# A gated mLSTM and mixture-of-experts layer on one core: row normalization on ScalarE, a shorter logarithm for the gates, other queues for the first loads, a third buffer for context rows

## The chip, the core and the metric

The kernel runs on one core of a Trainium2 chip. The core has five engines with a queue of instructions each: TensorE (PE in the profile; its weight loads are PEld), VectorE (DVE), ScalarE (ACT), GpSimd (POOL) and SyncE (SP). An engine takes its instructions in order and waits at each one until the semaphores that it needs have been raised. SP issues most transfers between the chip's memory (HBM) and the on-chip memory (SBUF); ACT and POOL can issue transfers as well. TensorE writes its products into PSUM, in tiles of which there are few.

The metric is the time of one execution on the device in microseconds (us), lower is better. The kernel before takes 3212.82 us, the median of 3 runs (3210.32 to 3215.99).

## What is computed

The input x has 8 sequences of 512 tokens of width 1024, and a context of the same shape. All is float32. With tokens in rows, for each sequence:

```
xn    = layernorm(x)                                   # over the 1024 columns
gates = [xn, ctx, ctx] @ [Wi | Wf] + [bi | bf]         # 16 input and 16 forget gates a token
logf  = log_sigmoid(forget gate); cum = cumsum(logf)   # along the sequence
D     = exp(cum_s - cum_t + i_t - max over t)          # t <= s, for each of 16 heads
C     = (xn_h @ ctx_h^T) / 8 * D                       # heads of width 64
h     = C / max(|sum C|, exp(-max)) @ ctx_h            # then normalized per head, scaled
x1    = x + tanh(g_xattn) * h
y     = layernorm(x1)
out   = x1 + tanh(g_ffn) * (shared(y) + routed(y))     # SwiGLU networks
```

`shared` is a SwiGLU network of width 1024 for all tokens; `routed` sends each token to the best 2 of 16 experts of width 512 by a router's softmax and sums their outputs with the two weights.

## The kernel before

The 4096 tokens are 32 tiles of 128 rows. The work has two parts, and the first is the one that the change touches.

**Attention part (lines 306 to 926, up to about 1450 us).** The loop at line 856 goes over the tiles i. One iteration holds pieces of three tiles: the last steps of tile i-1 (`head_norm`, `finish_rows`, `turn_rows`, routing), the scores and values of tile i, and the first steps of tile i+1 (`prep_queries`, `prep_keys`, `gate_products`, `prep_gates`, `prep_columns`), with the loads and the normalization of tile i+2. So that TensorE does not wait, units of the shared network for tiles already finished are laid between these pieces: `fill(share)` takes units from a queue, each 16 matmuls of 128x256 (lines 248) or half the down projection (line 265), about 7 us of TensorE for two of them.

The chain of a tile through the engines is this:

- The x row arrives by SP (line 321), the context row kv as well (line 326, two buffers).
- `row_stats` (lines 120 to 127): two `bn_stats` and one `bn_aggr` on DVE give mean and variance. `inverse_deviation` (lines 111 to 118): two operations on POOL give 1/sqrt(variance + eps). `normed` (line 426): one DVE operation subtracts the mean and multiplies. This is done for x (`prep_norm`) and again for x1 (`finish_rows`), 64 times in all.
- The normalized row is transposed on TensorE, eight 128x128 blocks in two PSUM tiles of tag "tr" (line 408), and copied out by ACT (qT, line 409). The same is done with kv, copied out by DVE (kT), and later with y (yT). Tag "tr" has two buffers, which these transposes share with the gates' products and `prep_columns`.
- `gate_products` and `prep_gates` (lines 455 to 525): the products `pp` are copied by ACT (`parts`, line 421), summed by one more matmul (`pg`, line 464), and worked on in 16x128 rows by DVE and ACT: the forget gate f (line 471), its bias (473), z = min(-f, f), exp(z) on ACT (478), u = 1 + exp(z), its logarithm on ACT (480), and then nine DVE operations (481 to 489). They correct the logarithm by z/(u - 1), which takes a reciprocal, and by a comparison for u = 1. Two scans give cum and the running maximum m, and nm = -m (line 501).
- nm goes to HBM and comes back broadcast to all partitions as the tile `d` (lines 505 and 506); exp of m goes the same way as `eb` (lines 513 to 520). POOL cuts the upper triangle of d (line 535).
- `prep_columns` transposes the gates' rows (`pc`, line 530); DVE copies them to `cols` (line 532), takes the decay out of eb (541) and multiplies eb by the queries (542). POOL forms wv (line 550).
- 16 exponentials on ACT (line 577), with cols as bias, turn d into D; DVE multiplies it with the scores (line 593); the values follow on TensorE (lines 608 and 614).

The order of the instructions on each engine is set by a scheduler when the program is built, from the order in the source and the tiles' dependences. `tc.issue_after(ins)` keeps what is written under it behind `ins`. `pinned(order, after)` does the same for an instruction handed on; `behind` holds the last matmul of the last unit of `fill`.

**Start (lines 86 to 424 and 810 to 851).** Constants are set on POOL; SP loads x and kv of tiles 0 and 1 and the input gates' weights `wi`; ACT's queue issues the loads of the two gates, `wf`, the two biases, `lnsc`, the router's weights and the zeros into the last rows of `acc_d`. Then the first tile goes through the chain alone.

**Expert part (lines 994 to 1446, from about 1450 us).** The experts' products, at line 1281, with the same instructions before and after.

Of the kernel before, what the change touches and what calls it, by code (L numbers as in the profile page):

```python
# [9 lines left out]
F32 = mybir.dt.float32  # L10
# [8 lines left out]
P = 128  # L19
S = 512  # L20
D = 1024
# [21 lines left out]
def flamingo_layer(  # L43
# [47 lines left out]
    mhalf = const.tile([P, NH], F32, name="mhalf")  # L91
    nc.gpsimd.memset(mhalf, -0.5)
    gates_t = const.tile([P, 2], F32, name="gates_t")
    nc.scalar.dma_start(gates_t[:, 0:1], g_xattn.unsqueeze(0).to_broadcast([P, 1]))
    nc.scalar.dma_start(gates_t[:, 1:2], g_ffn.unsqueeze(0).to_broadcast([P, 1]))
    tg = const.tile([P, 2], F32, name="tg")
    nc.scalar.activation(tg, gates_t, AF.Tanh)
    tgx, tgf = tg[:, 0:1], tg[:, 1:2]
# [21 lines left out]
    def row_stats(pool, row):  # L120

        st = pool.tile([P, 2, 6], F32, tag="bst", name="bst")
        for k in range(2):
            nc.vector.bn_stats(st[:, k, :], row[:, k * 512 : (k + 1) * 512])
        mv = pool.tile([P, 2], F32, tag="bmv", name="bmv")
        nc.vector.bn_aggr(mv, st.rearrange("p a b -> p (a b)"))  # L126
        return mv
# [178 lines left out]
    with ExitStack() as actx:  # L306
# [15 lines left out]

        def load_kv(i: int):
            q, b, c = toks[i], i // NS, i % NS
            q.kv = wk.tile([P, D], F32, tag="kv", name="kv")
            nc.sync.dma_start(q.kv, ctx_in[b, c * P : (c + 1) * P, :])

        load_x(0)
# [3 lines left out]

        w3 = wk.tile([P, 3 * NC, 32], F32, tag="sq", name="w3", bufs=1)
        nc.sync.dma_start(w3[:, :, 0:NH], wi.rearrange("(c p) h -> p c h", p=P))
        nc.scalar.dma_start(w3[:, :, NH:], wf.rearrange("(c p) h -> p c h", p=P))
        bias_i = ac.tile([NH, 1], F32, name="bias_i")
        bias_f = ac.tile([NH, 1], F32, name="bias_f")
        nc.scalar.dma_start(bias_i, bi.unsqueeze(1))
        nc.scalar.dma_start(bias_f, bf.unsqueeze(1))
        ones_p = ac.tile([P, P], F32, name="ones_p")  # L340
        nc.gpsimd.memset(ones_p, 1.0)
        ones = ones_p[:NH, :]
# [11 lines left out]
        ltop = ac.tile([P, 2, NT], F32, name="ltop")  # L354

        lnsc = ac.tile([P, D], F32, name="lnsc")
        nc.scalar.dma_start(lnsc, ln_scale.unsqueeze(0).to_broadcast([P, D]))


        sums = ac.tile([P, 48], F32, name="sums")  # L360
# [15 lines left out]
        state = ac.tile([P, NH // 2, 2 * (DH + 1)], F32, name="state")  # L376
        nc.gpsimd.memset(state, 0.0)
        zeros = state.rearrange("p c e -> p (c e)")
        nc.scalar.dma_start(acc_d[T : T + P, :], zeros[:, :D])
        zero80 = ac.tile([P, NT_], F32, name="zero80")  # L380
        nc.gpsimd.memset(zero80, 0.0)
        uptos = [ac.tile([P, 5, NE], F32, name=f"upto{k}") for k in range(2)]
# [10 lines left out]
        def prep_router():  # L393
            nc.vector.tensor_scalar(lnsc, lnsc, tgx, None, ALU.mult)
            rw = wk.tile([NE, D], F32, tag="u", name="rw", bufs=1)
            nc.scalar.dma_start(rw, router_w)
            nc.vector.memset(rwT, 0.0)
            prw = ps.tile([P, NC, NE], F32, tag="tr", name="prw")
            for c in range(NC):
                nc.tensor.transpose(prw[:, c, :], rw[:, c * P : (c + 1) * P], ident[:NE, :NE])  # L400
            nc.scalar.copy(rwT[:, :, 0:NE], prw)
# [19 lines left out]
            nc.scalar.copy(parts, pp)  # L421
            return parts

        def normed(row, mean, rstd):
            o = wk.tile([P, D], F32, tag="row", name="row", bufs=2)
            normed.last = nc.vector.tensor_scalar(o, row, mean, rstd, ALU.subtract, ALU.mult).ins
            return o

        def prep_norm(i: int):
            q = toks[i]  # L430
            mv = row_stats(sm, q.x)
            rstd = inverse_deviation(sm, mv[:, 1:2], LN_EPS, [P, 1])
            q.xn = normed(q.x, mv[:, 0:1], rstd)

        def prep_values(i: int):
            q = toks[i]
# [22 lines left out]
        def prep_gates(i: int, after=()):  # L459
            q, last, first = toks[i], i % NS == NS - 1, i % NS == 0  # L460
            pg = ps.tile([48, P], F32, tag="tr", name="pg")
            with ExitStack() as order:
                pinned(order, after)
                nc.tensor.matmul(pg, lhsT=sums, rhs=q.parts, start=True, stop=True)

            def row(name, bufs=2):
                return gt.tile([NH, P], F32, tag=name, name=name, bufs=bufs)

            f = row("f", 1)
            a, en, w = (rows3[i % 2][32 * k : 32 * k + NH, :] for k in range(3))  # L470
            nc.scalar.copy(f, pg[32:48, :])
            nc.vector.tensor_scalar(a, pg[0:NH, :], bias_i, None, ALU.add)
            nc.vector.tensor_scalar(f, f, bias_f, None, ALU.add)


            z, u, lnu, eq = (row(n, 1) for n in ("z", "u", "lnu", "eq"))
            nc.vector.scalar_tensor_tensor(z, f, -1.0, f, ALU.mult, ALU.min)
            nc.scalar.activation(z, z, AF.Exp)
            nc.vector.tensor_scalar(u, z, 1.0, None, ALU.add)
            nc.scalar.activation(lnu, u, AF.Ln)  # L480
            nc.vector.tensor_scalar(u, u, -1.0, None, ALU.add)
            nc.vector.tensor_scalar(eq, u, 0.0, None, ALU.is_equal)
            nc.vector.tensor_add(u, u, eq)
            nc.vector.reciprocal(u, u)
            nc.vector.tensor_mul(u, u, z)
            nc.vector.tensor_mul(lnu, lnu, u)
            nc.vector.tensor_mul(eq, eq, z)
            nc.vector.tensor_add(lnu, lnu, eq)
            nc.vector.scalar_tensor_tensor(f, f, 0.0, lnu, ALU.min, ALU.subtract)

            q.cum, q.m = row("cum"), row("m")
            before = None if first else toks[i - 1]
            nc.vector.tensor_tensor_scan(
                q.cum, ones, f, 0.0 if first else before.cum[:, P - 1 : P], ALU.mult, ALU.add
            )
            nc.vector.tensor_sub(a, a, q.cum)
            nc.vector.tensor_tensor_scan(
                q.m, a, a, LOWEST if first else before.m[:, P - 1 : P], ALU.max, ALU.max
            )
            nm = row("nm", 1)  # L500
            nc.vector.tensor_scalar(nm, q.m, -1.0, None, ALU.mult)
# [21 lines left out]
            nc.scalar.activation(en, en, AF.Exp, scale=-1.0)  # L523
            if not last:
                nc.scalar.activation(w, a, AF.Exp, bias=nm[:, P - 1 : P])

        def prep_columns(i: int):
            q, last, first = toks[i], i % NS == NS - 1, i % NS == 0
            pc = ps.tile([P, 5, NH], F32, tag="tr", name="pc")
            nc.tensor.transpose(pc.rearrange("p k h -> p (k h)"), rows3[i % 2], ident[:80, :80])  # L530
# [146 lines left out]
        def finish_rows(i: int):  # L677
            q = toks[i]
            nc.sync.dma_start(x1_d[i] if i < NT - 4 * HELD else acc_d[i * P : (i + 1) * P, :], q.x)
            mv = row_stats(sm, q.x)  # L680
            rstd = inverse_deviation(sm, mv[:, 1:2], LN_EPS, [P, 1])
            q.y = normed(q.x, mv[:, 0:1], rstd)
            nc.sync.dma_start(y_d[i * P : (i + 1) * P, :], q.y)

        def turn_rows(i: int):
# [126 lines left out]
        prep_norm(0)  # L812
        prep_queries(0)
        prep_keys(0)
        with tc.issue_after(normed.last):
            prep_gate_weights()
            prep_values(0)
        gate_products(0)
        prep_gates(0)
        prep_columns(0)  # L820
        with tc.issue_after(normed.last):
            prep_norm(1)
        with tc.issue_after(normed.last):
            prep_router()
        prep_weights(0, 0)
        prep_weights(0, 1)
# [16 lines left out]
        nc.sync.dma_start(sh_down, sh_down_w.rearrange("(c p) d -> p c d", p=P))  # L843
        prep_values(1)
        load_x(2)
        prep_columns(1)
        load_kv(2)
        route_products(0)
        finish_route(0)
        fill()  # L850
# [5 lines left out]
        for i in range(1, NT):  # L856
# [622 lines left out]
```

## Time and profile before

| What | Value |
|---|---|
| time, median of 3 runs | 3212.82 us |
| the profiled execution: time | 3221.06 us |
| its span, first to last instruction | 3219.3 us |
| granted TensorE clock, mean over the span | 0.975 |
| TensorE busy | 3107.8 us, 97% |
| VectorE busy | 1798.4 us, 56% |
| ScalarE busy | 863.7 us, 27% |
| GpSimd busy | 1295.2 us, 40% |

The profile is of one execution. Its page has, for each engine, the busy time and the number of instructions, the busy share in 40 equal slices, and the costliest groups of instructions by line of the code with their tiles as "out<-in". The trace behind it answers more: the busy time by stretch, the waits ("engine, line <- what it waited for: total us, times, longest us"), and the instructions in order of time. A wait for several semaphores is put down to the one that came last. Matmuls are pipelined and their ends are modelled, so short gaps of TensorE are not exact.

### The profile page before, as it was taken

What the parts mean: (1) busy time and instruction counts of PE and PEld (TensorE: products, weight loads), DVE (VectorE), ACT (ScalarE), POOL (GpSimd) and SP (SyncE); (2) the same over time, 40 slices, a digit from 0 to 9 for tenths busy, and PEclk for the clock granted to TensorE, in tenths of its full rate; (3) what the DMA queues carried; (4) which work ended last, traced back from release to release, by engine and by line L of the source; (5) the groups of instructions that cost most, each with busy time, mean ns of one, the idle gap of its engine ahead of it and who ended that gap; (6) DMA issues with size and microseconds to landing.
All of it is one profiled execution on the core that took longest, in us unless ns stands there. A gap on an engine that the chain in (4) does not pass through costs nothing.

```text
span 3219.3 us, 42324 instructions
## 1 busy us (share of the span) xinstructions
PE 3107.8 (97%) x16127; PEld 2294.8 (71%) x16127; DVE 1798.4 (56%) x3573; ACT 863.7 (27%) x1825; POOL 1295.2 (40%) x993
## 2 busy tenths in 40 slices
PE   6999989999999999999999999999999999999999
PEld 5778777786877867666666666666677777776666
DVE  5655666767667675644444444444454445455554
ACT  3444444443544544311111111111111111100000
POOL 2213232323231323235555555555565544444342
PEclk7889999999999999999999999999999999999999
DMA  6766565666656666553544545444454544645330
GB/s 191 206 210 190 174 181 171 191 187 187 197 170 191 184 188 174 161 198 130 141 121 115 141 134 136 122 119 128 129 142 135 141 129 131 187 163 173 106 130 27
DMA packets 371280, 501.52 MB, mean 156 GB/s; under 512 B 24352, under 2 KB 262480, under 8 KB 366944
## 3 DMA queue, kind: packets, MB, share of 16 engines
q1 hardware_dynamic: 342560, 425.00, 42.1%
q0 software_dynamic: 24752, 72.44, 10.8%
q8 instruction: 130, 2.13, 0.3%
q10 hardware_dynamic: 3760, 1.31, 0.2%
q14 instruction: 78, 0.64, 0.1%
HBM read 394.57 MB, written 114.61 MB: 158 GB/s over the span
## 4 chain that ended last, share of the span: by engine, by line
PE 51%; DVE 3%; issue 0%; DVEq 0%
PE pq L1281 48%; PE ptx L1199 2%; PE pq L1382 1%; DVE hsum L1345 1%; DVE hsum L1346 1%; DVE hT L1303 1%; DVE up L1302 0%; DVE tsum L1230 0%; DVE tsum L1228 0%; DVE tsum L1227 0%; DVE yo L1356 0%; DVE hT L1347 0%; DVE u L1363 0%; DVE u L1362 0%; DVE xT L1202 0%
## 5 line engine op out<-in xcount | busy, mean ns | idle before, releaser
L1281 PE MATMUL pq<-xT,w 128*128 128x256 f32 (+1 forms) x2112 | 513.4, 393 | 8.5 <-DVEq L1262 8.5
L1281 PEld LDWEIGHTS pq<-xT,w 128*128 128x128 f32 x2112 | 401.7, 191 | 101.3 <-issue 13.4
L1281 PE MATMUL pq<-tsum,wsum 128*128 128x256 f32 (+1 forms) x1408 | 349.8, 391 | 0.0
L248 PE MATMUL pgu<-sh_yT,swg 128*128 128x256 f32 (+1 forms) x1280 | 299.2, 384 | 1.3 <-DMA swg<-L_ffn_shared_gate_w_dram 1.3
L1281 PEld LDWEIGHTS pq<-tsum,wsum 128*128 128x128 f32 x1408 | 264.0, 190 | 49.5
L265 PE MATMUL pso<-sh_down,sh_hT 128*128 128x512 f32 x640 | 286.8, 599 | 2.3 <-DVE sh_hT L254 2.3
L248 PE MATMUL pgu<-sh_yT,swu 128*128 128x256 f32 (+1 forms) x1280 | 278.1, 371 | 0.9 <-DMA swu<-n_L_ffn_shared_up_w_dram 0.9
L248 PEld LDWEIGHTS pgu<-sh_yT,swu 128*128 128x128 f32 x1280 | 235.3, 191 | 31.5 <-DMA swu<-n_L_ffn_shared_up_w_dram 1.1
L1305 DVE TENSOR_TENSOR hT<-pq,u 128x256 f32<-128x256 f32 (+1 forms) x176 | 77.2, 439 | 322.4 <-PE pq L1281 318.8
L248 PEld LDWEIGHTS pgu<-sh_yT,swg 128*128 128x128 f32 x1280 | 233.1, 197 | 33.5 <-issue 3.2
L114 POOL TENSOR_SCALAR ve<-bmv 128x1 f32<-128x1 f32 x64 | 15.6, 243 | 580.7 <-DVE bmv L126 578.5
L1246 POOL TENSOR_TENSOR wsum<-w 128x512 f32<-128x512 f32 x88 | 113.6, 1290 | 295.1 <-PE pq L1281 290.8
L265 PEld LDWEIGHTS pso<-sh_down,sh_hT 128*128 128x128 f32 x640 | 119.0, 192 | 136.8 <-issue 132.1
L1302 DVE TENSOR_TENSOR up<-pq,u 128x256 f32<-128x256 f32 (+1 forms) x176 | 77.1, 438 | 223.7 <-PE pq L1281 222.3
L1012 POOL DMA_INDIRECT acc_d<-yo,row_i x64 | 102.1, 1595 | 184.4 <-ACT yo L1374 70.4
L1281 PE MATMUL pq<-wd,hT 128*128 128x512 f32 x352 | 169.6, 597 | 6.9 <-DVE hT L1303 5.4
L1281 PE MATMUL pq<-xT,wsum 128*128 128x256 f32 (+1 forms) x704 | 174.9, 391 | 0.0
L1281 PE MATMUL pq<-tsum,w 128*128 128x256 f32 (+1 forms) x704 | 174.9, 391 | 0.0
L1306 ACT ACTIVATE hT<-hT 128x256 f32<-128x256 f32 (+1 forms) x176 | 75.4, 429 | 339.2 <-DVE hT L1305 339.2
L1281 PE MATMUL pq<-dsum,hT 128*128 128x512 f32 x352 | 165.4, 592 | 0.0
L1281 PE MATMUL pq<-dsum,hsum 128*128 128x512 f32 x352 | 165.4, 592 | 0.0
L1356 DVE TENSOR_TENSOR yo<-pq,u 128x512 f32<-128x512 f32 x176 | 118.9, 686 | 76.9 <-PE pq L1281 56.5
(265 smaller groups left out, 5478.4 us busy)
## 6 DMA issues: line engine op xcount, KB each, us to landing
swg<-L_ffn_shared_gate_w_dram SPq DMA_DIRECT2D x88, 512.0 KB, 5.0
swu<-n_L_ffn_shared_up_w_dram SPq DMA_DIRECT2D x88, 512.0 KB, 5.8
w<-in_L_ffn_gate_w_dram SPq DMA_DIRECT2D x16, 2048.0 KB, 9.8
w<-in_L_ffn_up_w_dram SPq DMA_DIRECT2D x16, 2048.0 KB, 9.9
wd<-in_L_ffn_down_w_dram SPq DMA_DIRECT2D x16, 2048.0 KB, 8.0
d<-nm_d SPq DMA_DIRECT2D x31, 1024.0 KB, 6.2
x_sb<-in_x_dram SPq DMA_DIRECT2D x32, 512.0 KB, 4.9
kv<-in_ctx_dram SPq DMA_DIRECT2D x32, 512.0 KB, 6.0
```

The source lines that it names most:

```text
L248: last = nc.tensor.matmul(pg[:, half, :n], lhsT=w[:, c, :], rhs=st["yT"][:, c, :n], start=(c == 0), stop=(c == NC - 1),)
L265: last = nc.tensor.matmul(po, lhsT=st["hT"][:, k, t * P : (t + 1) * P], rhs=sh_down[:, k, cols], start=(k == 0), stop=(k == 2 * NFC - 1),)
L1012: nc.gpsimd.indirect_dma_start(out=rows, out_offset=bass.IndirectOffsetOnAxis(ap=index, axis=0), in_=row, in_offset=None, compute_op=ALU.add,)
L1199: nc.tensor.transpose(pt[:, c, :], row[:, (half * 4 + c) * P : (half * 4 + c + 1) * P], ident)
L1246: nc.gpsimd.tensor_tensor(s1, a21, a22, ALU.add)
L1281: nc.tensor.matmul(out, lhsT=left[:, c, :], rhs=right[:, c, :], start=(c == 0), stop=(c == chunks - 1))
L1302: nc.vector.tensor_tensor(up, part, other, ALU.add)
L1303: nc.vector.tensor_tensor(out, out, up, ALU.mult)
L1305: nc.vector.tensor_tensor(out, part, other, ALU.add)
L1306: nc.scalar.activation(out, out, AF.Silu)
L1345: nc.vector.tensor_tensor(s1, a21, a22, ALU.add)
L1356: nc.vector.tensor_tensor(rows[t][:, halves[half]], part, other, ALU.add)
```

## The change

- `normed` becomes one ACT activation, out = row * rstd + shift, with a new POOL operation for shift = -mean * rstd.
- The copy of f on ACT adds the bias. The correction of the logarithm becomes (u - 1 - z), subtracted from it: no division and no comparison. Ten DVE operations become three.
- The loads of the gates, biases, `lnsc`, the router's weights and the store of zeros are issued by POOL; `wf` by SP.
- kv has three buffers, and `load_kv(i + 2)` stands beside `load_x(i + 2)` in the middle of the iteration.
- At the end of the iteration `fill(share)` comes ahead of `prep_columns(i + 1)`, whose transpose is pinned behind the last unit.
- At the start, what was kept behind the first normalized row is kept behind its statistics, or behind nm of the first tile.

```diff
     def row_stats(pool, row):
         for k in range(2):
-            nc.vector.bn_stats(st[:, k, :], row[:, k * 512 : (k + 1) * 512])
+            row_stats.last = nc.vector.bn_stats(st[:, k, :], row[:, k * 512 : (k + 1) * 512]).ins
...
-    nc.scalar.dma_start(gates_t[:, 0:1], g_xattn.unsqueeze(0).to_broadcast([P, 1]))
-    nc.scalar.dma_start(gates_t[:, 1:2], g_ffn.unsqueeze(0).to_broadcast([P, 1]))
+    nc.gpsimd.dma_start(gates_t[:, 0:1], g_xattn.unsqueeze(0).to_broadcast([P, 1]))
+    nc.gpsimd.dma_start(gates_t[:, 1:2], g_ffn.unsqueeze(0).to_broadcast([P, 1]))
...
-            q.kv = wk.tile([P, D], F32, tag="kv", name="kv")
+            q.kv = wk.tile([P, D], F32, tag="kv", name="kv", bufs=3)
...
-        nc.scalar.dma_start(w3[:, :, NH:], wf.rearrange("(c p) h -> p c h", p=P))
+        nc.sync.dma_start(w3[:, :, NH:], wf.rearrange("(c p) h -> p c h", p=P))
-        nc.scalar.dma_start(bias_i, bi.unsqueeze(1))
-        nc.scalar.dma_start(bias_f, bf.unsqueeze(1))
+        nc.gpsimd.dma_start(bias_i, bi.unsqueeze(1))
+        nc.gpsimd.dma_start(bias_f, bf.unsqueeze(1))
-        nc.scalar.dma_start(lnsc, ln_scale.unsqueeze(0).to_broadcast([P, D]))
+        nc.gpsimd.dma_start(lnsc, ln_scale.unsqueeze(0).to_broadcast([P, D]))
-        nc.scalar.dma_start(acc_d[T : T + P, :], zeros[:, :D])
+        nc.gpsimd.dma_start(acc_d[T : T + P, :], zeros[:, :D])
-            nc.scalar.dma_start(rw, router_w)
+            nc.gpsimd.dma_start(rw, router_w)
...
-        def normed(row, mean, rstd):
+        def normed(row, mv):
+            rstd = inverse_deviation(sm, mv[:, 1:2], LN_EPS, [P, 1])
+            shift = sm.tile([P, 1], F32, tag="shift", name="shift")
+            nc.gpsimd.tensor_scalar(shift, mv[:, 0:1], rstd, -1.0, ALU.mult, ALU.mult)
             o = wk.tile([P, D], F32, tag="row", name="row", bufs=2)
-            normed.last = nc.vector.tensor_scalar(o, row, mean, rstd, ALU.subtract, ALU.mult).ins
+            nc.scalar.activation(o, row, AF.Identity, scale=rstd, bias=shift)
             return o
...
-            nc.scalar.copy(f, pg[32:48, :])
+            nc.scalar.activation(f, pg[32:48, :], AF.Identity, bias=bias_f)
             nc.vector.tensor_scalar(a, pg[0:NH, :], bias_i, None, ALU.add)
-            nc.vector.tensor_scalar(f, f, bias_f, None, ALU.add)
...
             nc.scalar.activation(lnu, u, AF.Ln)
-            nc.vector.tensor_scalar(u, u, -1.0, None, ALU.add)
-            nc.vector.tensor_scalar(eq, u, 0.0, None, ALU.is_equal)
-            nc.vector.tensor_add(u, u, eq)
-            nc.vector.reciprocal(u, u)
-            nc.vector.tensor_mul(u, u, z)
-            nc.vector.tensor_mul(lnu, lnu, u)
-            nc.vector.tensor_mul(eq, eq, z)
-            nc.vector.tensor_add(lnu, lnu, eq)
-            nc.vector.scalar_tensor_tensor(f, f, 0.0, lnu, ALU.min, ALU.subtract)
+            nc.vector.scalar_tensor_tensor(u, u, -1.0, z, ALU.add, ALU.subtract)
+            nc.vector.scalar_tensor_tensor(f, f, 0.0, u, ALU.min, ALU.add)
+            nc.vector.tensor_sub(f, f, lnu)
...
-        def prep_columns(i: int):
+        def prep_columns(i: int, after=()):
...
-            nc.tensor.transpose(pc.rearrange("p k h -> p (k h)"), rows3[i % 2], ident[:80, :80])
+            with ExitStack() as order:
+                pinned(order, after)
+                nc.tensor.transpose(pc.rearrange("p k h -> p (k h)"), rows3[i % 2], ident[:80, :80])
...
-        with tc.issue_after(normed.last):
+        with tc.issue_after(row_stats.last):
             prep_gate_weights()
             prep_values(0)
...
-        with tc.issue_after(normed.last):
+        with tc.issue_after(toks[0].gated):
             prep_norm(1)
-        with tc.issue_after(normed.last):
             prep_router()
...
             if i + 2 < NT:
                 load_x(i + 2)
+                load_kv(i + 2)
             fill(share)
...
-            if i + 2 < NT:
-                load_kv(i + 2)
+            fill(share)
             if nxt:
-                prep_columns(i + 1)
-            fill(share)
+                prep_columns(i + 1, behind)
```

(`toks[i].gated` is the instruction at line 501 that writes nm.)

More of the change, by code (lines that the diff above doesn't have):

```diff
@@ L430, in prep_norm @@
             q = toks[i]
-            mv = row_stats(sm, q.x)
-            rstd = inverse_deviation(sm, mv[:, 1:2], LN_EPS, [P, 1])
-            q.xn = normed(q.x, mv[:, 0:1], rstd)
+            q.xn = normed(q.x, row_stats(sm, q.x))
         def prep_values(i: int):
@@ L470, in prep_gates @@
             a, en, w = (rows3[i % 2][32 * k : 32 * k + NH, :] for k in range(3))
-            nc.scalar.copy(f, pg[32:48, :])
+            nc.scalar.activation(f, pg[32:48, :], AF.Identity, bias=bias_f)
             nc.vector.tensor_scalar(a, pg[0:NH, :], bias_i, None, ALU.add)
-            nc.vector.tensor_scalar(f, f, bias_f, None, ALU.add)
-            z, u, lnu, eq = (row(n, 1) for n in ("z", "u", "lnu", "eq"))
+            z, u, lnu = (row(n, 1) for n in ("z", "u", "lnu"))
             nc.vector.scalar_tensor_tensor(z, f, -1.0, f, ALU.mult, ALU.min)
@@ L500, in prep_gates @@
             nm = row("nm", 1)
-            nc.vector.tensor_scalar(nm, q.m, -1.0, None, ALU.mult)
+            q.gated = nc.vector.tensor_scalar(nm, q.m, -1.0, None, ALU.mult).ins
             q.d = wk.tile([P, NH, P], F32, tag="d", name="d")
@@ L679, in finish_rows @@
             nc.sync.dma_start(x1_d[i] if i < NT - 4 * HELD else acc_d[i * P : (i + 1) * P, :], q.x)
-            mv = row_stats(sm, q.x)
-            rstd = inverse_deviation(sm, mv[:, 1:2], LN_EPS, [P, 1])
-            q.y = normed(q.x, mv[:, 0:1], rstd)
+            q.y = normed(q.x, row_stats(sm, q.x))
             nc.sync.dma_start(y_d[i * P : (i + 1) * P, :], q.y)
@@ L845, in flamingo_layer @@
         load_x(2)
+        load_kv(2)
         prep_columns(1)
-        load_kv(2)
         route_products(0)
```

## The prediction

> **What bounds the kernel now.** I read the page first, then the busy time by stretch, then TensorE's waits in each stretch, then single iterations in the timeline. The page (busy by engine, then slices):
>
> ```profile
> PE 3107.8 (97%) x16127; PEld 2294.8 (71%) x16127; DVE 1798.4 (56%) x3573; ACT 863.7 (27%) x1825; POOL 1295.2 (40%) x993
> ...
> PE   6999989999999999999999999999999999999999
> ...
> PEclk7889999999999999999999999999999999999999
> ```
>
> TensorE (PE) is the bound, and the change leaves its work as it is: the same matmuls, in another order. So it can win or lose only PE's idle time, and the clock that PE is granted near it. The busy times by stretch say how much there is:
>
> ```profile
> 0.00:80.00 80.00, 50.36 (x354) 44.71 (x355) 43.27 (x100) 24.88 (x55) 17.66 (x45) 0.72 0.66 190
> 80.00:320.00 240.00, 222.56 (x1694) 187.55 (x1692) 146.60 (x321) 106.45 (x244) 58.84 (x48) 0.90 0.71 204
> 320.00:1340.00 1020.00, 982.44 (x6770) 755.63 (x6769) 699.08 (x1541) 462.59 (x1038) 278.24 (x238) 0.98 0.62 182
> 1340.00:1453.00 113.00, 99.90 (x485) 73.93 (x481) 52.88 (x170) 19.46 (x40) 32.14 (x31) 0.94 0.56 187
> 1453.00:3219.00 1766.00, 1752.52 (x6832) 1232.95 (x6832) 856.55 (x1442) 250.32 (x450) 908.30 (x632) 1.00 0.46 130
> ```
>
> Columns: stretch, length, busy us of PE, its weight loads, DVE, ACT and POOL, then the granted clock. PE is idle 80 - 50.4 = 29.6 us at the start, 17.4 in the first tiles, 37.6 in the steady attention part (about 24 iterations of 42 us), 13.1 at its end and 13.5 in the expert part. The change touches the first three alone: 84.6 us. PE's waits, first of the start, then of the steady part (total, times, longest):
>
> ```profile
> PE pt L408 <- DVE row L426: 17.7, 2, 9.3
> PE pm L564 <- DVE nm L501: 7.9, 1, 7.9
> PE pt L408 <- ACT qT L409: 3.0, 1, 3.0
> ```
>
> ```profile
> PE pt L408 <- DVE row L426: 6.8, 6, 2.2
> PE pt L408 <- DMA kv<-in_ctx_dram: 6.2, 5, 2.5
> PE pc L530 <- ACT rows L523: 5.5, 2, 5.1
> PE pl L707 <- ACT parts L421: 5.4, 3, 3.2
> PE pp L416 <- ACT yT L409: 3.1, 2, 2.0
> ```
>
> There is no one stall to remove in the steady part: some twenty of 0.3 to 5 us. DVE is 69% busy there, and its queue is in order, so small delays on DVE are what these waits are made of.
>
> **Norm on ScalarE.** Two normalized rows a tile leave DVE, 64 in all. The nearest row for the new place is an ACT scale of a 128x1024 row by a column; min/median/max in ns:
>
> ```profile
> L426 DVE TENSOR_SCALAR row<-x_sb,bmv,rstd x64: 779/812/870, 8.5 to 1389.3; 128x1024 f32<-128x1024 f32 x64
> ```
>
> ```profile
> L1374 ACT ACTIVATE yo<-yo,wslot x64: 1147/1148/1151, 1526.1 to 2773.2; 128x1024 f32<-128x1024 f32 x64
> ```
>
> A bias column adds about 0.09 (L525 with one takes 398 ns, L523 without 308, both 16x128), so I take 1.24 us; at the least two 512-wide ACT copies less their start, about 1.1, at the most 1.3. POOL also gains the shift, one more operation like L114's 222 ns. A row alone is thus 0.24 + 1.24 - 0.81 = 0.7 us later. But DVE no longer stands still for POOL's root (waits of DVE on rstd: 62.9 us up to 1300 us, the longest 7.3), and ACT does so instead. In the built order of ACT the y row stands behind the copy of the gate parts and ahead of f, and the next x row ahead of the copy of the router's parts. ACT has room: 462.6 of 1020 us busy, plus 2.5 a tile. Table loads, counted in the built order, go from 174 to 164; none stands at the new activation.
>
> The Trainium skill speaks against this part: "ScalarE: Activation LUTs", Rules for kernel authors, sends adds and multiplies to VectorE. The two rows above agree that ScalarE is slower, 1148 to 812 ns; by the rule alone the sum would be 64 x 0.34 = 21 us worse, by the rows it is nothing while ACT's idle time covers it.
>
> **Gates without division.** Out go L473 (266 ns), L481 to L489 (215, 215, 280, 941, 267, 278, 216, 278, 278); in come three of about 280. f with a bias column costs ACT 0.09 more. That is 3.23 - 0.84 = 2.4 us less for DVE a tile, and about 2.9 less on the chain from f to nm, since two of the new three can run beside the logarithm on ACT. With the two rows DVE loses 2.4 + 1.6 = 4.0 of 42 us a tile, from 69% to 59% busy. The chain from f to nm, 14.2 us at the median, is mostly queueing on DVE. Worked through the tile whose gate product ends at 854.9: the y row ends on ACT at about 857.5, f at 857.9, exp, a table load of 1.28 and ln by 861, three short operations, two scans and nm at 862.6, against 867.5 before. I take the chain as 3 to 5 us earlier.
>
> **Start.** Seven loads go to POOL's queue (two gates, two biases, lnsc, zeros, router); wf goes to SP, ahead of x and kv of tile 1. In the built order six of them stand ahead of POOL's first `ve`, and the router's load between `ve` and the root. The trace has no plain load issued by POOL: an indirect one takes 0.97 us of POOL (L999, L787), a scatter 1.60, an issue on ACT's queue 0.41. I take 0.97. POOL's own setup takes 3.9 us, so the root ends at 0.3 + 3.9 + 7 x 0.97 + 1.5 = 12.5 instead of 8.4, and the first row at 13.9 instead of 9.3: 4.5 us late. The kv transposes follow at 15.9 instead of 14.3 only, since the 3.0 us in which ACT's queue held back qT for its loads are gone; the gate product is 1.6 late. From f to nm: 5.5 us instead of 8.8 (no other work between them in DVE's new order). Sum: 1.6 - 3.3 = -1.7; the exponentials then stand behind the second row on ACT, which costs what the earlier nm leaves. I take -3 with the shorter y(0) chain; with 0.41 or 1.60 a load, -7 or +2.
>
> The skill's "DMA: Bandwidth & Descriptors", SWDGE vs HWDGE vs iDMA, gives plain transfers to SP or ACT, since GpSimd builds its descriptors in software. By that rule these loads are in the wrong place and only the delayed row counts, +4.5; by the rows the freed ACT queue pays most of it back.
>
> **Third kv buffer.** SP waited 19.1 us at the start, and 39.3 us in 13 places later, for a matmul to free the kv tile. The load now stands half an iteration earlier, so PE's kv waits go: 6.2 + 1.3 = 7.5 us; I take -7 (0 to -7.5). Its cost is SBUF, 4 KB a partition.
>
> **Columns behind the unit.** `prep_columns` moves behind the last filler matmuls of an iteration. Its waits go (pc on rows 5.5, pt on cols 1.9: -7). But its PSUM tile shares two buffers with the row transposes, which now follow at once: the second half of them waits for DVE's copy `cols`. With DVE free that copy is done 0.5 us after pc starts (29.41 to 30.03 at the first tile with its waits; 77.27 to 77.81), about when the first four transposes end: 0.1 us x 31. In some 12 tiles a 0.74 us PSUM operation of the filler stands ahead of the copy: +0.4 each. Together +8. And in 21 tiles the built order now has the copy of the decay and its product (0.17 + 1.23) ahead of `cols`, and these wait for the eb DMA. With the times of before, that is the slower rival below; with a chain 3 us earlier it costs 8, with 4 us 3. I take +5. Part: -7 + 8 + 5 = +6.
>
> **The rest.** DVE stalls behind which PE waits (state 7.2, d and hT 4.5 up to 1340 us) shrink with DVE's load; I take -6 (0 to -12). Rows and router parts (11.5 and 5.4) I leave: later by ACT, earlier by DVE. Fewer idles early on mean less time at the reduced clock (0.90 there): -2 (0 to -10).
>
> **Sum.** -3 - 7 + 6 - 6 - 2 = -12 us. The profiled execution took 3221.06 (span 3219.3 and 1.8 around it), 8.2 above the median 3212.82; from its own time this makes 3209, and for the median **3201**. I say 3200.
>
> **Rivals.** (1) *The columns' copy becomes the wait: slower.* If the gate chain is no earlier, the decay's wait for eb stands ahead of `cols`, and PE stands behind it. With decay's start in before, 1.66 us to the end of `cols` and the start of the transposes plus 0.65, 13 of 21 tiles stall, 36 us together; at 2 us earlier still 16. Price: -3 - 7 + 1 + 36 = +27, 3240; it decides from a chain less than 3 us earlier. For it: SP's new order has a weight load, which waits for PE, between the e_d store and the loads of d and eb. Against: DVE's lighter load. (2) *Idle only moves: no change.* The row waits by 0.7 us more at PE in a third of the tiles, the router's parts stand behind a row on ACT, and these (11.5 + 5.4, doubled less half) eat the kv gain: about -2, 3211. (3) *Queues untangle: larger gain.* If the waits of the steady part halve (-19), the first tiles' too (-9), the start is at its good end (-7) and the clock follows (-5): -40, 3173. (4) *POOL's loads decide the start*: at 1.6 us or more each, with f to nm no shorter, +5 to +9 and no other gain: 3220.
>
> **Numbers.** Forecast 0.40 (3190 to 3206); larger gain 0.15; no change 0.15 (3206.4 to 3219.2, 0.2% either way, about what a measurement of this kernel can tell); columns' wait 0.22; POOL's loads 0.08. So faster 0.55, same 0.15, slower 0.30. Both signs weigh: the range reaches from rival 3's end to rival 1's, 3174 to 3238.
>
> **What would show it.** Steps right: PE's kv wait gone; first transposes of rows at about 14 us, nm by 26; f to nm near 9 us at the median; DVE 9 to 10 points less busy from 320 to 1340. Wrong: a new line "pt from cols" or "DVE decay from DMA" of over 15 us; PE's busy time itself changed by over 10 us, which this sum does not expect; an idle POOL at 10 us.

## The result, and the profile after

The changed kernel takes 3237.94 us (median of 4, 3234.21 to 3243.96), the kernel before beside it 3214.40: a ratio of 1.0074, 95% interval 1.0052 to 1.0096, slower by some 24 us. The forecast of 3200 had the sign wrong; the time lies at the very end of the stated range (3238), beside the rival "the columns' copy becomes the wait" (3240).

The profiled execution took 3243.96 us, 22.9 more than that of before. From its page, the engines' busy time, then TensorE's slices and its clock:

```profile
PE 3109.1 (96%) x16127; PEld 2293.1 (71%) x16127; DVE 1653.4 (51%) x3285; ACT 934.1 (29%) x1879; POOL 1318.9 (41%) x1064
...
PE   5889999899998999998999999999999999999999
...
PEclk6899999999999999999999999999999999999999
```

PE's own work is the same (3107.8 before), and DVE does 145 us less. So only PE's idle time and its clock can have made the difference. The busy times by stretch (stretch, length, busy us of PE, its weight loads, DVE, ACT and POOL, then the granted clock):

```profile
0.00:80.00 80.00, 46.94 (x312) 39.51 (x313) 36.68 (x81) 27.62 (x56) 21.79 (x54) 0.68 0.62 189
80.00:320.00 240.00, 214.32 (x1654) 181.10 (x1654) 125.63 (x267) 116.15 (x248) 62.39 (x57) 0.92 0.70 195
320.00:1340.00 1020.00, 967.77 (x6608) 745.16 (x6607) 566.44 (x1280) 505.20 (x1052) 284.68 (x282) 0.97 0.61 180
1340.00:1453.00 113.00, 113.00 (x665) 86.69 (x664) 61.93 (x207) 31.57 (x68) 22.23 (x24) 1.00 0.46 146
1453.00:3240.00 1787.00, 1767.12 (x6894) 1240.66 (x6892) 862.74 (x1452) 253.56 (x456) 927.79 (x648) 1.00 0.46 134
```

DVE fell from 69% to 56% busy in the steady part, more than forecast. PE's idle time nevertheless rose: 29.6 to 33.1 us at the start, 17.4 to 25.7 in the first tiles, 37.6 to 52.2 in the steady part; up to the expert part from 88.4 to 111.0 us. Tile by tile, the gate product pg of tile 8 is 7 us later than before, that of tile 18 24 us, that of tile 30 34 us; the expert part then begins 24 us late and takes as long as before. PE's waits of the steady part:

```profile
PE pt L408 <- DVE cols L530: 26.3, 11, 5.4
PE pl L703 <- ACT parts L421: 12.1, 6, 4.1
PE pso L265 <- DVE sh_base L270: 6.4, 2, 6.0
PE pt L408 <- ACT row L430: 6.3, 5, 1.9
PE psc L584 <- DVE state L644: 1.0, 2, 0.7
```

The first line was 1.9 us in the kernel before, and another 7.3 us of it lie in the first tiles. It is the line that the prediction named as a sign against itself ("pt from cols" of over 15 us). So is the first of DVE's waits of the same part, here of before and then of after:

```profile
DVE decay L541 <- DMA eb<-e_d: 40.5, 11, 8.6
DVE decay L539 <- DMA eb<-e_d: 111.2, 16, 13.2
```

How the two hang together shows in one iteration, in order of time (start, duration, what ran, in brackets the idle time before it and its releaser):

```profile
816.18 0.17 DVE L539 COPY decay<-eb 128x8 f32<-128x8 f32 x1 [12.20 <-DMA eb<-e_d]
816.39 1.22 DVE L540 SCALAR_TENSOR_TENSOR eb<-eb,qT 128x1024 f32<-128x1024 f32 x1
...
819.18 1.21 DVE L657 TENSOR_REDUCE var<-sq 128x16 f32<-128x1024 f32 x1
...
821.87 0.23 PE L528 MATMUL pc<-ident,rows 80*128 80x80 f32 x1
821.94 0.60 PE L408 MATMUL pt<-ident,row 128*128 128x128 f32 x4
...
822.34 0.43 DVE L644 TENSOR_TENSOR state<-state,pst 64x260 f32<-64x260 f32 x1
...
825.79 1.22 DVE L442 TENSOR_REDUCE vmean<-kv 128x16 f32<-128x1024 f32 x1 [3.02 <-DMA kv<-in_ctx_dram]
827.04 0.21 DVE L530 COPY cols<-pc 128x48 f32<-128x48 f32 x1
...
827.30 1.11 PE L408 MATMUL pt<-ident,row 128*128 128x128 f32 x4 [4.76 <-DVE cols L530]
```

DVE stands for 12.20 us until eb lands. What piled up behind (values, head variance, state additions) takes it to 822.8. Then the reduction `vmean` (of the context rows two tiles on) stands 3.02 us until kv lands, and only then comes `cols`. PE had put the columns into pc at 821.87 and waits with the second half of the row transposes for that buffer. In the built order of after, the decay stands ahead of `cols` in 22 of the 24 tiles that have one, and a `vmean` at most ten operations ahead of it in 15 of 32; in that of before in 2 and 1.

The start, PE's waits (before: row 17.7, nm 7.9, qT 3.0):

```profile
PE pt L408 <- ACT row L430: 14.9, 3, 12.4
PE psc L584 <- DVE state L642: 9.8, 2, 8.2
PE pm L562 <- DVE nm L497: 4.3, 1, 4.3
```

### The profile page after: what moved, and what is told of

Same layout as the page of the kernel before. It is cut to its first block, busy times and chain, and to the rows that moved or that the text cites. A ratio compares the mean times of both kernels' runs of the same rounds, so it can differ in the third digit from the quotient of the medians.

```text
span 3242.2 us, 42202 instructions
## 1 busy us (share of the span) xinstructions
PE 3109.1 (96%) x16127; PEld 2293.1 (71%) x16127; DVE 1653.4 (51%) x3285; ACT 934.1 (29%) x1879; POOL 1318.9 (41%) x1064
## 3 DMA queue, kind: packets, MB, share of 16 engines
q0 software_dynamic: 25200, 73.55, 10.9%
## 4 chain that ended last, share of the span: by engine, by line
PE 51%; DVE 3%; issue 0%; DVEq 0%
PE pq L1275 48%; PE ptx L1193 2%; PE pq L1376 1%; DVE hsum L1339 1%; DVE hsum L1340 1%; DVE hT L1297 1%; DVE up L1296 0%; DVE tsum L1224 0%; DVE tsum L1222 0%; DVE tsum L1221 0%; DVE yo L1350 0%; DVE hT L1341 0%; DVE u L1357 0%; DVE u L1356 0%; DVE xT L1196 0%
## 5 line engine op out<-in xcount | busy, mean ns | idle before, releaser
L660 POOL TENSOR_TENSOR hrstd<-var,mhalf 128x16 f32<-128x16 f32 x32 | 93.5, 2922 | 165.3 <-DVE var L658 165.2
```

The costliest lines, as they stand in the source:

```text
L660: nc.gpsimd.tensor_tensor(q.scale, var, mhalf, ALU.pow)
```

## Experiments

Each ratio is against the kernel before, from repeated executions of both on one chip, with its 95% interval; 0.001 is 3.2 us. The kernel before had medians of 3213 to 3221 us in these comparisons, so the times that are forecast below are read as ratios to the 3214 us of the first comparison.

| kernel | ratio | interval |
|---|---|---|
| columns' move alone | 1.0088 | 1.0056 to 1.0119 |
| rows on ScalarE alone | 1.0046 | 1.0026 to 1.0067 |
| gates without division alone | 1.0054 | 1.0036 to 1.0072 |
| third kv buffer, earlier load alone | 0.9974 | 0.9959 to 0.9989 |
| first loads alone | 1.0001 | 0.9985 to 1.0017 |
| gates, loads and kv together | 1.0000 | 0.9984 to 1.0016 |
| after, columns' move undone | 1.0050 | 1.0026 to 1.0073 |
| after, rows back on VectorE | 1.0106 | 1.0075 to 1.0137 |
| after, pc in other PSUM buffers | 1.0028 | 1.0012 to 1.0044 |
| after, decay held behind cols | 0.9987 | 0.9969 to 1.0005 |
| after, vmean held behind cols | 1.0039 | 1.0023 to 1.0055 |
| after, both held | 0.9973 | 0.9959 to 0.9987 |
| after, decay held, vmean held from tile 8 | 0.9943 | 0.9923 to 0.9964 |
| the same, rows on VectorE | 1.0005 | 0.9986 to 1.0024 |
| after, decay held, rows on VectorE | 1.0033 | 1.0018 to 1.0048 |
| columns alone, decay held | 1.0092 | 1.0067 to 1.0117 |
| columns alone, decay held, vmean from tile 8 | 1.0035 | 1.0018 to 1.0052 |
| kv and columns, decay held | 1.0067 | 1.0042 to 1.0092 |

The theory after the first look (C): `cols` is late behind a DMA wait on DVE's queue, and PE stands behind `cols`. The rivals: the rows on ScalarE cost it (N), and the early kv load moves vmean ahead of `cols` (S).

**1. The columns' move alone.**

```diff
+            fill(share)
             if nxt:
-                prep_columns(i + 1)
-            fill(share)
+                prep_columns(i + 1, behind)
```

> The kernel before with one part alone: the gates' columns moved behind the filler matmuls. Theory C (the columns' copy on VectorE stands behind the decay, which waits for the eb load, and TensorE's row transposes wait for the copy's PSUM buffer): slower by 20 to 40 us against before, with a new TensorE wait pt from cols of 25 us or more in the attention part. Theory N (the rows on ScalarE cost it: gates' f, router parts and the stores behind them): within 8 us of before, pt from cols under 10 us. Theory S (the early kv load lets the reduction for the next values stand ahead of cols, so the move is harmless without it): 0 to +10 us.

+0.88%, and of PE's waits in the steady part:

```profile
PE pt L408 <- DVE cols L534: 32.4, 15, 6.4
PE pl L709 <- ACT parts L421: 10.1, 4, 4.1
```

As C has it, in time and wait; whether the eb load is the reason is asked in edit 13. S falls: vmean stands close ahead of `cols` in 15 tiles here too, without the early load.

**2. After, with that move undone** (the same lines the other way round).

> The kernel after with the columns' move alone undone. Theory C: faster than the kernel before, 3200 to 3212 us, the wait pt from cols gone, and pc from rows back with about 5 us. Theory N: 3228 to 3240, still slower than before. Theory S: 3208 to 3220, as the kv reduction no longer stands ahead of cols.

1.0050. This is in N's range (3228 to 3240 us are 1.004 to 1.008) and above those of C and S, so C's forecast missed. The wait pt from cols is not gone either (7.5 us), and pc from rows is not back. By the ratios the undoing gives back a third of the loss, in intervals that overlap: the move is not the whole. DVE stands for eb here too, 96.4 us in 17 places.

**3. The rows on ScalarE alone** (`normed`, its two callers, and the two places that named its last instruction).

```diff
-            normed.last = nc.vector.tensor_scalar(o, row, mean, rstd, ALU.subtract, ALU.mult).ins
+            nc.scalar.activation(o, row, AF.Identity, scale=rstd, bias=shift)
```

> The kernel before with the rows' normalization on ScalarE alone. Theory C: -10 to +5 us. Theory N: +12 to +30 us, with TensorE waiting for the router's parts and for rows by over 10 us more than before. The prediction's own step put it near 0.

+0.46%, some 15 us, as N has it; PE's waits for rows in the steady part are 23.7 us, in the kernel before 6.8. TensorE's idle time up to the expert part is 15.5 us longer than before, as much as its two longest waits for a row have together: 7.41 us up to 624.4, and 8.12 up to 1128.0, which the trace shows as follows.

```profile
1115.07 1.10 POOL L787 DMA_INDIRECT table_d<-rowid,slots_i  x1 [13.15 <-DVE slots_i L784]
...
1124.32 0.97 POOL L787 DMA_INDIRECT table_d<-rowid,slots_i  x1 [0.30 <-issue]
1125.37 0.24 POOL L114 TENSOR_SCALAR ve<-bmv 128x1 f32<-128x1 f32 x1
1125.70 0.57 POOL L117 TENSOR_TENSOR rstd<-ve,mhalf 128x1 f32<-128x1 f32 x1
1126.37 0.27 POOL L428 TENSOR_SCALAR shift<-bmv,rstd 128x1 f32<-128x1 f32 x1
1126.67 1.24 ACT L430 ACTIVATE row<-x_sb,shift,rstd 128x1024 f32<-128x1024 f32 x1 [9.16 <-POOL shift L428]
...
1127.97 1.33 PE L408 MATMUL pt<-ident,row 128*128 128x128 f32 x5 [8.12 <-ACT row L430]
```

The statistics were ready at 1115.7; the row's root (`rstd`) stood behind eight indirect transfers of the routing table, 10.2 us on GpSimd, and so waited 9.7 us. The other place looks the same. This is read from the trace; a run with the two exchanged was not made. In after the same eight come first too, but the statistics are ready late among them, and the root's chain waits 3.5 us (1139.4 to 1143.0); PE's waits for rows are 6.3 us in all.

**4. After, with the rows back on VectorE.**

```diff
-            nc.scalar.activation(o, row, AF.Identity, scale=rstd, bias=shift)
+            nc.vector.tensor_scalar(o, row, mv[:, 0:1], rstd, ALU.subtract, ALU.mult)
```

> The kernel after with the rows' normalization put back on VectorE. Theory C: no better than after, 3235 to 3255, since VectorE is busier and the gate chain later, so the columns' copy is too. Theory N: 3205 to 3222.

1.0106, as C has it. N falls as the explanation of after: with the rows back on VectorE the loss stays. That it is slower than after is not shown, since the two intervals overlap.

**5. After, pc in other PSUM buffers.**

```diff
-            pc = ps.tile([P, 5, NH], F32, tag="tr", name="pc")
+            pc = ps.tile([P, 5, NH], F32, tag="o", name="pc")
```

> The kernel after, with the columns' PSUM tile pc taken from the buffers of the filler's and the router's products (tag o) instead of from those that the row transposes use (tag tr); order of the parts unchanged. Theory C (TensorE stalls because its row transposes want the PSUM buffer that the late copy cols must free): the wait pt from cols (26.3 us in the steady part of after) falls below 3, TensorE's idle time up to the expert part falls from 111 to about 85 to 95, and the time to 3205 to 3222. Theory D (VectorE as a whole is late there; cols is only the first to show it): the same idle comes back as waits for kT, scores' d or sh_base, time 3228 to 3240.

1.0028, just above C's range (3222 us is 1.0025). The wait pt from cols is gone, and PE's idle time falls from 111.0 to 99.5 us, not to the 95 or less that C gave. PE's waits for sh_base rise from 6.4 to 11.8 us, those for rows from 6.3 to 11.0, and those of the scores for state from 1.0 to 7.4. Half C, half D: the shared buffer passes DVE's lateness to PE, which is worth some 15 of the 24 us, and part of the lateness finds another way.

**6. After, the decay held behind cols.**

```diff
+                with tc.issue_after(q.copied):
                     nc.vector.tensor_copy(q.decay, q.eb[:, :, P - 1])
                     nc.vector.scalar_tensor_tensor(
```

(`q.copied` is the copy `cols`.)

> The kernel after, with the decay's copy and product held behind the copy cols in VectorE's order, nothing else changed. If the wait for the eb load ahead of cols is what delays it (the prediction's rival): pt from cols under 8 us, time 3208 to 3222. If the rest of VectorE's queue ahead of cols is the larger part (state additions, head variance, and the reduction vmean that waits for the kv load): pt from cols still 12 to 25 us, time 3224 to 3240.

0.9987, a time of the first forecast with a wait of the second. This order alone is worth some 28 us, more than the change lost, and PE's idle time up to the expert part is 90.3 us, about that of before (88.4). DVE's wait for eb falls from 111.2 to 1.9 us. Of the gain only some 10 us pass through pt from cols (33.6 to 23.2 us with the first tiles); the wait for sh_base (6.4) is gone as well, so the stand for eb had held up other work of DVE too. What is left of pt from cols, and one of DVE's waits that tells why:

```profile
PE pt L408 <- DVE cols L530: 18.1, 7, 5.5
```

```profile
DVE vmean L442 <- DMA kv<-in_ctx_dram: 18.9, 12, 4.8
```

**7. Gates, loads and kv together** (rows and columns as before).

> The kernel before with three of the five parts: gates without division, first loads on the other queues, third kv buffer with the earlier load; rows stay on VectorE, columns stay where they were. If the columns' move and the rows on ScalarE are all of the loss: 3190 to 3212, faster than before. If one of these three parts costs as well: 3218 to 3235.

1.0000, between the two forecasts: what kv gains (edit 11) is lost again, and the loads (edit 12) do not lose it. The gates alone lose more (edit 8), so the three do not add up.

**8. Gates without division alone.**

```diff
-            nc.vector.reciprocal(u, u)
...
+            nc.vector.scalar_tensor_tensor(u, u, -1.0, z, ALU.add, ALU.subtract)
+            nc.vector.scalar_tensor_tensor(f, f, 0.0, u, ALU.min, ALU.add)
+            nc.vector.tensor_sub(f, f, lnu)
```

> The kernel before with the gates' logarithm without division alone. By the prediction's sum: -3 to -12 us against before, from f to nm shortened by 3 to 5 us. If a shorter chain only moves the idle time: within 5 us of before.

+0.54%, some 17 us and outside both forecasts, though f to nm fell from 14.2 to 10.6 us at the median. The idle time sits in many small places (router parts from yT 9.3, rows 7.8, parts 6.4, kv 6.1, cols 5.2); no run here takes them apart. One thing that the text above ties to the columns' move is here without it: the decay stands ahead of `cols` in 10 tiles, and DVE waits 108.0 us for eb, in the kernel before 40.5. By itself that need not cost: edit 7 has the same 10 tiles and 83.3 us of this wait, and loses nothing.

**9 and 10. After, vmean held behind cols; then both.**

```diff
+            with ExitStack() as order:
+                if i > 1:
+                    order.enter_context(tc.issue_after(toks[i - 1].copied))
                 nc.vector.reduce_sum(mean, heads, AX.X)
```

> The kernel after, with the reduction vmean of a tile's context rows held behind the previous copy cols in VectorE's order; the decay stays ahead of cols. It tells apart two waits ahead of cols: for the kv load (vmean) and for the eb load (decay). If the kv wait is worth about as much as the eb wait: 3218 to 3232, pt from cols 26 to about 15 us. If only the eb wait counts: 3232 to 3242, pt from cols over 20 us.

> The kernel after, with the decay, its product and the reduction vmean all held behind the copy cols. If these two waits are all that makes cols late: pt from cols (18.1 us with the decay alone held) under 8 us in the steady part, time 3196 to 3210, below the kernel before. If the state additions and the head variance ahead of cols are late by themselves: pt from cols over 12 us, time 3208 to 3222.

1.0039 and 0.9973, both in the first forecast: each wait counts, eb's more. The hold of the decay is clear of the intervals; that of vmean (11 us alone, 4 on top of the other) is not quite, and edit 15 shows it better. Summed over the steady part, `cols` starts 40 us behind pc in after, 25 and 24 us with one of the two held, 11 with both; pt from cols is then 3.9 us. The gate product of tile 8, though, is now 16.5 us later than before's (in after 7.0).

**11. The kv part alone** (the buffer and the two moved calls).

> The kernel before with the third kv buffer and its earlier load alone. The prediction's step: -7 us (0 to -7.5) against before, TensorE's waits for the kv load (6.2 us in the steady part) gone. Rival: the earlier load lets vmean move up in VectorE's order to where it waits for the load, and the gain is lost: 0 to +12 us.

0.9974, -8.4 us: the size of the prediction's step, and PE's waits for kv are gone. But PE's waits in the steady part for rows (12.7 us, in the kernel before 6.8) and for cols (5.7, there 1.9) have grown, and its idle time up to the expert part is 86.8 us, 1.6 less than before's. Where the 8 us come from is thus not shown.

**12. The first loads alone.**

> The kernel before with the first loads on the other queues alone. The prediction's step: within 5 us of before (the first row late by 4.5 us at the predicted 0.97 us of GpSimd a load, about 2 with the 0.55 seen in after; ScalarE's queue freed by 3.0). Rival: GpSimd's loads decide the start, +5 to +9 us.

1.0001, within its 5 us.

**13. The columns' move alone, with the decay held** (edits 1 and 6).

> The kernel before with the columns' move and the decay held behind the copy cols in VectorE's order; nothing else. If the eb wait ahead of cols is what made the move alone slower by 0.88%: the loss falls to between -0.2 and +0.3% against before. If the move is dear by the rest (the row transposes behind cols at once, state additions ahead of it): still +0.5 to +0.9%.

1.0092, the second forecast: nothing gained. DVE's wait for eb (22.5 us in edit 1) is 5.3, but the one for kv has gone from 7.8 to

```profile
DVE vmean L440 <- DMA kv<-in_ctx_dram: 36.4, 14, 7.6
```

So the wait ahead of `cols` changed its name only.

**14. After, the decay held, rows on VectorE** (edits 4 and 6).

> The kernel after with the decay held behind cols, and the rows' normalization back on VectorE. If the rows on ScalarE cost by themselves, as they did alone (+0.46%): faster than the same kernel with rows on ScalarE (0.9987 of before), at 0.993 to 0.997. If the cost of the rows alone was an accident of the order that the scheduler made there: 0.997 to 1.004.

1.0033 where rows on ScalarE gave 0.9987: the second forecast.

**15. After, the decay held, vmean from tile 8 on** (edit 9 with `i > 7`).

> The kernel after with the decay held behind cols from the start, and the reduction vmean from the eighth tile on. With both held from the start the first six tiles lost 16 us against before and the later ones won 23; if the loss is from holding vmean there, this keeps the gain without it: 0.990 to 0.995 of before. If the early loss is of other parts: 0.996 to 1.000.

0.9943, 3193.24 us against 3213.29: the first forecast and the fastest kernel here. Its first tiles and its steady part, and PE's waits in the latter:

```profile
80.00:320.00 240.00, 221.44 (x1765) 187.64 (x1764) 127.48 (x278) 124.15 (x262) 63.36 (x60) 0.96 0.74 208
320.00:1340.00 1020.00, 1000.92 (x6896) 775.03 (x6896) 617.83 (x1359) 520.36 (x1091) 287.33 (x289) 0.98 0.63 186
```

```profile
PE pt L408 <- ACT row L430: 9.8, 5, 2.3
PE pl L707 <- ACT parts L421: 4.6, 5, 2.8
PE pt L408 <- DVE cols L533: 2.8, 1, 2.8
```

PE is idle 19.1 us in 320 to 1340, half of before's 37.6. So the gain that the change aimed at was there, behind the two waits.

**16. kv and columns, decay held, rows and gates as before.**

> The kernel before with the third kv buffer and its earlier load, the columns' move, and the decay held behind cols. The kv part alone gave 0.9974. If the held move is harmless: 0.994 to 0.999. If vmean ahead of cols, which the early kv load brings, delays it: 1.000 to 1.005.

1.0067; pt from cols 17.1 us, vmean's wait for kv 23.4. This is on the side of the second forecast and above it, and the reverse of a harmless move.

**17. The columns' move alone, both held.**

> The kernel before with the columns' move alone (+0.88%), the decay held behind cols from the start and the reduction vmean from the eighth tile on. If cols is late by whichever DMA wait stands ahead of it (eb or kv), and by nothing else: 0.994 to 1.002 of before, pt from cols under 8 us in the steady part. If the move itself is dear on a VectorE that still writes the rows: 1.005 to 1.010.

1.0035, between the two forecasts: of the 0.88% the two waits are 0.53. Pt from cols is down to 2.0 us in the steady part (5.2 more in the first tiles); what is left shows as waits for rows (8.7) and kv (8.4).

**18. Edit 15 with the rows on VectorE.**

> The kernel of the last call's best run (0.9943 of before: after, decay held behind cols, vmean from the eighth tile on) with the rows' normalization back on VectorE. If the rows on ScalarE are a gain once cols waits for no DMA: 0.996 to 1.001. If they cost, as alone: 0.989 to 0.993.

1.0005 against 0.9943, the first forecast. With `cols` free, the rows on ScalarE gain 0.6%.

## Why the prediction was wrong

**Columns behind the unit: the step that failed.** The prediction knew the danger, and priced it away: "With the times of before, that is the slower rival below; with a chain 3 us earlier it costs 8, with 4 us 3. I take +5." The chain came 6.9 us earlier (f to nm 14.2 to 7.3 at the median), so by that rule nothing should have been left. Yet PE waited 33.6 us for `cols` (26.3 + 7.3), near the rival's full 36, and the part alone costs +28 us, not +6. Three things were left out. First, with the shorter chain DVE gets to the wait earlier as well. Counted from the end of a tile's pg, at the median of the steady part, DVE is free for the decay after 17.6 us in after and 26.1 in the kernel before, while the decay starts after 23.3 and 28.4; so the wait for eb grew from 40.5 to 111.2 us instead of going away. It is 83 to 108 us in edits 2, 7 and 8 as well, which shorten the gates and leave the columns in place, and 22.5 us with the columns moved alone. Second, the count ended with the decay and its product (0.17 + 1.23) as if `cols` came next; in the built order the values, the head variance, the state additions and vmean follow, and in the iteration shown `cols` starts 10.9 us after the decay. Third, vmean brings another DMA wait, for kv, which the working never met, though the order showed it in 15 tiles.

That DVE's waits for DMA ahead of `cols` cost after its loss is shown: holding the decay behind the copy, and vmean from tile 8 on, turns 1.0074 into 0.9943 (edits 6, 9, 10 and 15). That it goes by way of the shared buffer is shown for part of it (edit 5). Of the loss of the move alone, 0.35% stay when both are held (edit 17). Rival 1 named the right wait, but the point from which it was to decide, a chain less than 3 us earlier, was wrong. That its price of +27 came so near the 24 measured is therefore in part luck, and so is a range that ends at 3238, two short of that price. What spoke for the rival, the weight load in SP's order, did not matter: the second load of eb is issued 2.7 us after the store to e_d at the median, 3.1 in the kernel before.

**Third kv buffer: the size right.** -7 forecast, -8.4 alone (-13.2 to -3.5). PE's waits for kv went as forecast; that the gain is theirs is not shown, since other waits took their place (edit 11).

**Start: no gain, and off in its terms.** The loads alone give +0.3 us (-4.8 to +5.5), within the step's 5. But the sum had -3 for the start, and PE's idle time in the first 80 us is 3.5 us longer than before; by the gate product of tile 2 the two kernels are level. A plain load took 0.49 to 0.76 us of GpSimd, not 0.97, so the first row came at 11.12 and its transposes at 12.41, not 14. But DVE's copy of kT stood behind the values of tile 1, whose kv landed at 15.66, so the gate product was 2.4 us late, not 1.6. From f to nm 5.3 us, as forecast (5.5); nm at 27.3, where it was to be there by 26.

**Rows on ScalarE: the duration right, the price wrong.** 1240 ns a row, as taken; no table load. The sum had 0. It is +15 us alone, and a gain of about 20 (edit 18 against 15) once `cols` is free. In the run alone, the two longest waits come from the place of a row's chain on GpSimd, and the prediction looked at ScalarE's queue, not at GpSimd's.

**Gates and DVE's relief: -6 did not come.** The chain and DVE's load fell by more than forecast in after, and the gates alone cost 17 us. Taking an average (DVE's load) for a term failed: PE's idle time rose while the load fell. The order counts for more: edit 15 changes nothing else in after and wins 42 us. That the order also makes the price of the gates is likely, but not shown. The five parts alone add up to +52 us (28 + 15 + 17 - 8 + 0), all together give +24. Sums of parts do not hold here.

**Clock: not settled.** Over the whole profiled execution PE worked 119.9 us at half clock in after and 125.6 in the kernel before; by an estimate that is 3 us less, where -2 was forecast. But in the steady part the time at half clock rose from 48.4 to 61.4 us, and PE's busy time, over the same matmuls, by 1.3 in all. Executions of the kernel before differ by more than this among themselves (mean clocks of 0.974 to 0.988), so one trace of each does not tell.

Open: where the loss of the gates alone arises, and why the first tiles lose some 16 us when vmean is held from the start.

## What to carry to other kernels

Before a step is moved, read in the built order what stands ahead of its result on the in-order engine that frees the buffer, down to the last wait for a DMA, and count the whole pile behind that wait, not its first two instructions. A copy that TensorE waits for goes ahead of work that waits for DRAM; here holding the decay and a reduction behind it turned +0.74% into -0.57%. A shorter chain does not shorten a wait when the engine that waits gets there earlier too: take both ends from the new order. And where a scheduler builds the order, test each part both alone and left out: the price of the rows changed sign with its neighbours.

## What the runs showed of the hardware

A long stall of TensorE is paid twice. After the gap of 4.57 us that `cols` ended at 435.2 in after, the granted clock falls (last column but two: PEclk):

```profile
430.00:434.00 4.00, 0.65 (x6) 0.41 (x4) 3.92 (x11) 0.97 (x2) 2.92 (x1) 1.00 0.74 212
434.00:438.00 4.00, 2.78 (x20) 2.36 (x20) 1.32 (x7) 1.76 (x2) 1.93 (x1) 0.68 0.01 4
438.00:442.00 4.00, 4.00 (x23) 3.56 (x22) 2.86 (x5) 3.99 (x15) 0.00 (x0) 0.90 0.00 0
442.00:446.00 4.00, 4.00 (x20) 3.54 (x19) 3.90 (x5) 0.91 (x4) 0.00 (x0) 1.00 0.43 129
```

The records show the clock as 1.0 or 0.5, in steps of 3.41 us. Over the steady parts of all 20 traces, a gap above 2.5 us was followed by a stretch at 0.5 (one that begins in the gap or within 3 us after it) in 101 of 102 cases, one of 1.5 to 2.5 us in 49 of 84, one of 0.4 to 1.5 us in 21 of 231. Such a stretch lasts 5.6 to 6.4 us at the mean. After the gaps above 2.5 us PE is busy for 5.3 us of it, at half clock, so by an estimate such a gap costs 2.6 us besides itself.

The Trainium skill's "TensorE: Matmul & The Clock Gate", HAM oscillation — how this bites in real kernels, gives the rule of no TensorE gaps over about 3.4 us. The traces agree in kind and put the edge lower: gaps of 1.5 to 2.5 us did it in over half of the cases.

This is how one execution can lose without idling longer: in the profiled one with the columns' move undone (edit 2), the steady part's idle time is that of before (37.7 to 37.6), but its time at half clock is 75.1 us against 48.4. The clock differs between executions of one kernel, too: the twelve of edit 2 have mean clocks of 0.969 to 0.983, and the lowest goes with the longest time, 3244 us, the highest with the shortest, 3215.
